# Zero products ahead of the first image, and one step of the last half image moved from VectorE to Pool

## The chip, the cores and the metric

The kernel is one program on one core of a Trainium2 chip. The metric is the time of one execution on the device in microseconds (us); the median of several executions is compared. The names of the engines are those of the profile: PE (TensorE matmul) with PEld (its weight loads), DVE (VectorE), ACT (ScalarE), POOL (GpSimd) and SP (SyncE, which here only issues DMAs).

## The reference, cut to what matters

Four layers follow one another on x of shape (8, 512, 32, 32), in float32. The first layer's f and g products and its batch normalization over all eight images are the start of the program; the fourth layer is its end.

```python
# layer 0: the parts that the start of the kernel computes
f_x = relu(batchnorm(conv1x1(x, Wf, bf), gamma_f, beta_f)).reshape(b, MID, hw)   # MID = 64
g_x = relu(batchnorm(conv1x1(x, Wg, bg), gamma_g, beta_g)).reshape(b, MID, hw)
h_x = conv1x1(x, Wh, bh).reshape(b, MID, hw)
z = einsum('bcn,bcm->bnm', f_x, g_x)
attn = z / svd(z)[:, 0]
x = conv1x1(einsum('bnm,bcm->bcn', attn, h_x), Wv, bv) + x
# layer 1: group norm, attention over 1024 positions with 512 channels, projection, + x
# layer 2: attention over 1024 positions with 128 channels, projection, batchnorm, + x
# layer 3
a = sign(x + rsign_bias)
y = einsum('bchw,oc->bohw', a, sign(W) * mean(abs(W), axis=1))
s = batchnorm(y) + x
t = s - pr_shift
out = where(t > 0, t, pr_slope * t) + pr_bias
```

## The kernel before

An image is held as a tile `xt` of 128 partitions by 4 channel chunks by 1024 positions, 2 MB. Two such tiles exist (pool `x`, two buffers), so the load of the third image waits until PE is done with the first.

**The start.** f's and g's weights (`fg`, four DMAs of 64 KB) are issued on ACT's queue, the first image on SP's queue (`load_x(0, True)`, line 141: its first chunk in two halves of 256 KB, three chunks of 512 KB), then h's weights on ACT's queue (line 156). `ident` and other constants follow: Pool makes `ident`, DVE derives masks from it (lines 178 to 195), and ACT's queue loads a table `ct` of small vectors (line 201), from which DVE computes scales (lines 243 to 248 and 1309 to 1326).

In the loop over the eight images (line 1370) PE multiplies the f, g and h weights, 64 columns each, with the image: `products(i, cc)` (line 1382) takes weight set i and channel chunk cc, and puts the two halves of the positions side by side on the partitions of one PSUM bank. For the first image the chunks come outermost, and each chunk is used for f and g as it lands; h follows. Every such product of the code stands as two passes in the trace. The results go to SBUF by ACT (f, line 1401, and h, line 1410) and DVE (g, line 1404). PSUM has two wide tiles and four banks here (`psum_pools(early, 2, 4)`); `bank()` hands the four out in turn.

Within this loop a scheduler orders each engine's instructions by readiness in its own model of time, starting from the order of the text; `tc.keep_in_program_order(ins)` pins an instruction behind the one that precedes it in the text on the same engine. On PE the stretch after the loop is ordered by hand (`manual_schedule`).

**The middle.** Each image then passes layers 1 to 3 in `fast`; the last image has a path of its own at the end.

**The tail.** `leave` computes layer 3, for halves h = 0 and h = 1 of the positions. ACT takes the signs of the half's four chunks (line 720), PE multiplies them with the weights' signs (line 732). For the last image `signs` holds the unpacked signs; then each j in 0, 1 gives two pieces of 128 channels by 512 positions, `y1` (channels oc = j) and `y2` (oc = j + 2). DVE forms y = product x scale + x (line 753). From there two forms exist:

- for h = 0, and for j = 0 of h = 1: DVE takes `up` = max(y, nc3) x ps3 (line 759), ACT overwrites y with slope x y + bias (line 762), Pool adds the two (line 769), SP sends y out (line 770). ACT's overwriting waits until line 759 has read y.
- for j = 1 of h = 1: ACT takes a Relu into `up` (line 775) and the scaled y (line 776), DVE joins them (line 783), SP sends them out (line 787); the last piece goes in two halves.

Of the kernel before, what the change touches and what calls it, by code (L numbers as in the profile page):

```python
# [8 lines left out]
F32 = mybir.dt.float32  # L9
# [7 lines left out]
P = 128  # L17
# [70 lines left out]
def kernel(  # L88
# [17 lines left out]
    nc = tc.nc  # L106
    mm = nc.tensor.matmul
# [17 lines left out]
    def bank():  # L125
        return psum["bank"].tile([P, HF], F32, tag="bank", name="bank")
# [9 lines left out]
    def load_x(b, split=False):  # L136
        t = xpool.tile([P, CC, N], F32, tag="x", name="xt")
        src = x[b].rearrange("(cc p) n -> p cc n", p=P)
        for cc in range(CC):
            for ns in [half(h) for h in range(NH)] if split and not cc else [slice(0, N)]:  # L140
                nc.sync.dma_start(out=t[:, cc, ns], in_=src[:, cc, ns])
        return t

    def half(i):
        return bass.ts(i, HF)

    def side(i):

        return slice(i * MID, (i + 1) * MID)
# [4 lines left out]
    def load_w(name, src, shape, pool=wpool, eng=nc.sync, tag=None):  # L154
        t = pool.tile(shape, F32, tag=tag or name, name=name)
        eng.dma_start(out=t, in_=src)
        sbw[name] = t
        return t
# [4 lines left out]
    a1 = early.enter_context(tc.tile_pool(name="a1", bufs=1))  # L163
    fg = sbw["fg"] = a1.tile([P, CC, P], F32, tag="fg", name="fg")
    for cc in range(CC):
        nc.scalar.dma_start(out=fg[:, cc, :], in_=w_fg[:, cc, :])
    first = load_x(0, True)
    load_w("h", w_h, [P, CC, MID], a1, nc.scalar)


# [64 lines left out]
    def col(name, i):  # L235
        return ct[:, COL[name] + i : COL[name] + i + 1]
# [476 lines left out]
    def leave(env, xt, dst, halves=range(NH), signs=None, stop=False):  # L713


        small = env["small"]
        for h in halves:
            sg = env["e"].tile([P, CC, HF], F16, tag="e", name="sg")
            for cc in range(CC):
                nc.scalar.activation(  # L720
                    sg[:, cc, :], xt[:, cc, half(h)], AF.Sign, bias=rb3[:, cc : cc + 1]
                )
            if stop:
                yield
            for j in range(CC // 2):
                both = env["e"].tile([P, 2, HF], F32, tag="e", name="both")
                y1, y2 = both[:, 0, :], both[:, 1, :]

                def product(lt):
                    ps = bank()  # L730
                    for cc in range(CC):
                        mm(  # L732
                            out=ps,
                            lhsT=lt[:, cc, bass.ts(j, P)],
                            rhs=sg[:, cc, :],
                            start=cc == 0,
                            stop=cc == CC - 1,
                        )
                    return ps

                if signs is None:
                    ps = product(sw3)
                    nc.scalar.activation(y2, ps, AF.Identity, bias=round3, scale=1.0 / PACK)
                    nc.vector.tensor_scalar(y2, y2, ROUND, None, ALU.subtract)
                    nc.vector.scalar_tensor_tensor(y1, y2, -PACK, ps, ALU.mult, ALU.add)
                    sums = y1, y2
                else:
                    sums = [product(signs[0])]
                    yield
                    sums.append(product(signs[1]))  # L750

                for y, ps, oc in ((y1, sums[0], j), (y2, sums[1], j + 2)):
                    nc.vector.scalar_tensor_tensor(
                        y, ps, sa3[:, oc : oc + 1], xt[:, oc, half(h)], ALU.mult, ALU.add
                    )
                    up = small.tile([P, HF], F32, tag="half_a", name="up3")
                    if signs is not None and (h == 0 or j == 0):

                        nc.vector.tensor_scalar(
                            up, y, nc3[:, oc : oc + 1], ps3[:, oc : oc + 1], ALU.max, ALU.mult  # L760
                        )
                        nc.scalar.activation(
                            y,
                            y,
                            AF.Identity,
                            bias=qb3[:, oc : oc + 1],
                            scale=col("L3_conv_pr_slope", oc),
                        )
                        nc.gpsimd.tensor_tensor(y, y, up, ALU.add)
                        nc.sync.dma_start(out=dst[:, oc, half(h)], in_=y)  # L770
                        continue
                    final = signs is not None and y is y2
                    for q in (slice(0, HF // 2), slice(HF // 2, HF)) if final else [slice(0, HF)]:
                        yq, uq = y[:, q], up[:, q]
                        nc.scalar.activation(uq, yq, AF.Relu, bias=cb3[:, oc : oc + 1])
                        nc.scalar.activation(
                            yq,
                            yq,
                            AF.Identity,
                            bias=pb3[:, oc : oc + 1],  # L780
                            scale=col("L3_conv_pr_slope", oc),
                        )
                        nc.vector.scalar_tensor_tensor(
                            yq, uq, ps3[:, oc : oc + 1], yq, ALU.mult, ALU.add
                        )
                        to = slice(h * HF + q.start, h * HF + q.stop)
                        nc.sync.dma_start(out=dst[:, oc, to], in_=yq)
                yield
# [551 lines left out]
    def load_blocks(name, src, parts):  # L1340

        if name not in sbw:
            sbw[name] = a1.tile([P, 4, GROUPS, QUAD], F32, tag=name, name="blocks_" + name)
        t = sbw[name]
        of = src.rearrange("(r a) c o -> r a c o", a=QUAD)
        for q in range(4):
            for r in parts:
                nc.sync.dma_start(
                    out=t[bass.ts(q, QUAD), r].rearrange("a (c m) b -> a c (m b)", c=CC),
                    in_=of[r][:, :, bass.ts(q, P)],  # L1350
                )
# [18 lines left out]
    for b in range(B):  # L1370
        xt = load_x(b) if b else first
        for name, src, pool in later.get(b, ()):
            load_w(name, src, shapes.get(name, [P, CC, C]), pool)
        if b in (2, 3, 4, 5):
            load_blocks(*((("q", w_q), ("k", w_k))[b // 2 - 1]), ((0, 1), (2, 3))[b % 2])
        if b >= B - 2:
            resident[b] = xt
        banks = [bank() for _ in w0[: 3 if b < B - 2 else 2]]

        def products(i, cc):  # L1380
            for h in range(NH):
                mm(  # L1382
                    out=banks[i][side(h), :],
                    lhsT=w0[i][:, cc, :],
                    rhs=xt[:, cc, half(h)],
                    start=cc == 0,
                    stop=cc == CC - 1,
                )

        if b == 0:  # L1390
            for cc in range(CC):
                for i in range(2):
                    products(i, cc)
        for i in range(3):
            if i == 2 and b >= B - 2:
                continue
            if b or i == 2:
                for cc in range(CC):
                    products(i, cc)
            if i == 0:  # L1400
                nc.scalar.copy(fs[b], banks[i])
                nc.vector.bn_stats(st[:, 0, b, :], fs[b])
            elif i == 1:
                nc.vector.tensor_copy(gs[b], banks[i])
                nc.vector.bn_stats(st[:, 1, b, :], gs[b])
                if last is not None:
                    turn(last[0], last[1], ht_pair[last[0] // 2], 0)
        if b < B - 2:
            hraw = a2.tile([P, HF], F32, tag="hraw", name="hraw")
            nc.scalar.activation(hraw, banks[2], AF.Identity, bias=bhc)  # L1410
            last = b, hraw
        else:
            last = None
        if b == 3:
            total3 = sign_weights()
        if b == 5:
            scale_signs(total3)
        if b > 5:
            natural(*((("q", "w3"), ("k", "q"))[b - 6]))
# [165 lines left out]
    with tc.manual_schedule(engines={mybir.EngineType.PE}):  # L1585
# [7 lines left out]
        ps = bank()  # L1593
# [6 lines left out]
        ps = bank()  # L1600
# [233 lines left out]
```

## Time and profile before

| what | us |
|---|---|
| four runs | 1872.57 to 1873.49, median 1873.09 |
| the profiled execution | 1873.44 |
| its span, first to last instruction | 1871.7 |
| PE busy | 1851.9 |
| DVE busy | 1121.6 |
| ACT busy | 542.0 |
| POOL busy | 121.9 |
| first product of the first image (line 1382) | starts at 4.53 |
| end of the last line 783 | 1867.1 |

How to read it: the page gives the busy time of every engine as a share of the span, and the chain of work that ended last, followed back from the last instruction: 96% of that chain is PE. The view in order of time lists instructions with start and length in us, merged where like ones follow one another, and in brackets the engine's idle time before them with what ended it; "issue" there is idle time that no wait in the profile explains. The same chain of waits can be had as a list in order of time. A windows view adds up each engine's busy time and the bytes moved in chosen stretches.

### The profile page before, as it was taken

Reading aid. Unit: us, or ns where it says so; the run is one execution under the profiler, and the core shown is the slowest. Engines: PE = TensorE matmul, PEld = TensorE weight load, DVE = VectorE, ACT = ScalarE, POOL = GpSimd, SP = SyncE. Lnnn points to the kernel's source line nnn. Section 1 sums busy time; section 2 is a strip of 40 time slices with the busy share of each in tenths; the row PEclk is TensorE's granted clock in tenths of the full one; section 3 lists DMA queues with packets and bytes.
Section 4 is the critical chain, followed back from the end, with each engine's and each line's share of the span. In section 5 each row is a group of like instructions: output and inputs, shape, how many; then the busy total and the mean of one; then the engine's idle time right before and its main releaser. Section 6 shows DMA issues by size and latency. Waiting matters only on the chain.

```text
span 1871.7 us, 16535 instructions
## 1 busy us (share of the span) xinstructions
PE 1851.9 (99%) x6196; PEld 947.9 (51%) x6196; DVE 1121.6 (60%) x2083; ACT 542.0 (29%) x882; POOL 121.9 (7%) x109
## 2 busy tenths in 40 slices
PE   9999999999999999999999999999999999999997
PEld 3365464544645465544645455544645464544653
DVE  3356677567754667567754776357643666355447
ACT  2042221244213521244202521244203521244114
POOL 1000001000010001100020001100010001000011
PEclk9999999999999999999999999999999999999999
DMA  8620000002000200002000200001000200000001
GB/s 276 206 87 7 1 18 1 1 34 73 12 1 12 90 17 1 0 35 73 12 1 12 90 18 0 1 34 68 12 0 12 90 12 0 1 34 23 12 0 47
DMA packets 32738, 66.52 MB, mean 36 GB/s; under 512 B 4944, under 2 KB 12300, under 8 KB 32524
## 3 DMA queue, kind: packets, MB, share of 16 engines
q1 hardware_dynamic: 31724, 64.96, 10.2%
q8 instruction: 51, 0.84, 0.2%
q10 hardware_dynamic: 864, 0.43, 0.1%
q14 instruction: 35, 0.29, 0.1%
q0 software_dynamic: 64, 0.00, 0.0%
HBM read 46.44 MB, written 18.94 MB: 35 GB/s over the span
## 4 chain that ended last, share of the span: by engine, by line
PE 96%; DVE 2%; ACT 1%; issue 0%; DMA 0%; POOL 0%; ACTq 0%; DVEq 0%
PE bank L413 46%; PE bank L591 21%; PE bank L993 6%; PE bank L840 6%; PE bank L1382 4%; PE bank L692 3%; PE bank L709 3%; PE bank L732 1%; PE bank L437 1%; PE wide L1428 1%; PE bank L1061 1%; PE bank L1486 1%; PE quad L1274 0%; PE bank L863 0%; DVE st L449 0%; DVE xt L446 0%
## 5 line engine op out<-in xcount | busy, mean ns | idle before, releaser
L591 PE MATMUL bank<-e,vt 128*128 128x512 f32 x768 | 336.2, 594 | 0.0
L591 PEld LDWEIGHTS bank<-e,vt 128*128 128x128 f32 x768 | 144.3, 190 | 172.3 <-issue 167.9
L413 PE MATMUL bank<-ut,h 128*128 128x512 f32 x384 | 178.9, 597 | 0.0
L413 PEld LDWEIGHTS bank<-ut,h 128*128 128x128 f32 x384 | 71.2, 190 | 94.7 <-issue 93.0
L413 PE MATMUL bank<-us,hs 128*128 128x512 f32 x256 | 115.6, 593 | 0.0
L840 PE MATMUL bank<-tpg 128*128 128x512 f32 x256 | 115.4, 595 | 0.0
L993 PE MATMUL bank<-e,tpg 128*128 128x512 f32 x256 | 114.7, 595 | 0.0
L364 DVE TENSOR_TENSOR e<-bank,e 128x512 f32<-128x512 f32 x96 | 66.2, 689 | 60.8 <-PE bank L413 45.1
L847 ACT ACTIVATE e<-bank 128x512 f32<-128x512 f32 x128 | 76.3, 597 | 67.0 <-PE bank L840 66.9
L358 ACT COPY e<-bank 128x512 f32<-128x512 f32 x96 | 56.1, 585 | 118.9 <-PE bank L413 118.5
L413 PE MATMUL bank<-wo,h 128*128 128x256 f32 x384 | 89.9, 384 | 0.0
L413 PE MATMUL bank<-h,wu 128*128 128x512 f32 x192 | 89.0, 594 | 0.8 <-DVE h L488 0.8
L244 POOL TENSOR_TENSOR r_r<-r_v,minus_half 128x4 f32<-128x4 f32 (+1 forms) x11 | 10.9, 989 | 1042.7 <-DVE r_v L243 1037.4
L993 PEld LDWEIGHTS bank<-e,tpg 128*128 128x128 f32 x256 | 48.1, 190 | 60.4 <-issue 60.0
L413 PEld LDWEIGHTS bank<-wo,h 128*128 128x128 f32 x384 | 71.4, 190 | 12.6 <-issue 3.8
L413 PEld LDWEIGHTS bank<-us,hs 128*128 128x128 f32 x256 | 48.4, 190 | 57.5 <-issue 54.5
L852 DVE TENSOR_TENSOR esum<-esum,e 128x1024 f32<-128x1024 f32 x48 | 58.8, 1225 | 30.1 <-ACT e L847 29.9
L840 PEld LDWEIGHTS bank<-tpg 128*128 128x128 f32 x256 | 47.6, 190 | 55.0 <-issue 52.4
L720 ACT ACTIVATE sg<-xt,rb 128x512 f16<-128x512 f32 x64 | 44.2, 716 | 107.4 <-DVE xt L711 104.5
L364 DVE TENSOR_TENSOR vt<-bank,vt 128x512 f32<-128x512 f32 x48 | 33.2, 692 | 66.4 <-PE bank L413 65.6
L358 ACT COPY vt<-bank 128x512 f32<-128x512 f32 x64 | 37.4, 584 | 121.3 <-PE bank L413 121.2
L358 ACT COPY ut<-bank 128x512 f32<-128x512 f32 x48 | 28.1, 586 | 127.9 <-PE bank L413 127.9
(361 smaller groups left out, 2916.8 us busy)
## 6 DMA issues: line engine op xcount, KB each, us to landing
xt<-in_x SPq DMA_DIRECT2D x55, 512.0 KB
out<-both SPq DMA_DIRECT2D x63, 256.0 KB
rfull<-r_dram SPq DMA_DIRECT2D x15, 512.0 KB
f_dram<-f SPq DMA_DIRECT2D x8, 256.0 KB
fb<-f_dram SPq DMA_DIRECT2D x8, 256.0 KB
w<-in_w SPq DMA_DIRECT2D x1, 1024.0 KB
blocks_q<-in_w_q SPq DMA_DIRECT2D x16, 64.0 KB
blocks_k<-in_w_k SPq DMA_DIRECT2D x16, 64.0 KB
```

Source lines behind the costliest of these rows:

```text
L358: nc.scalar.copy(dst, ps)
L364: nc.vector.tensor_tensor(dst, ps, u, ALU.add)
L413: mm(out=ps[:, q * w : (q + 1) * w], lhsT=lt(ka, kb, q, k), rhs=rhs(ka, kb, q, k), start=first and q == 0 and k == 0, stop=last and k == 1 ...
L591: mm(out=ps, lhsT=a[:, t, bass.ts(r_, P)], rhs=e[t], start=first and t == 0, stop=last and t == NTH - 1, skip_group_check=True,)
L692: mm(out=ps[:, i, :], lhsT=xt[:, cc, bass.ts(4 * h + i, P)], rhs=sbw["tpg"][:, cc, 2 * P : 3 * P], start=cc == 0, stop=cc == CC - 1,)
L709: mm(out=ps, lhsT=sbw["z"][:, bass.ts(oc, P)], rhs=att, start=True, stop=True)
L720: nc.scalar.activation(sg[:, cc, :], xt[:, cc, half(h)], AF.Sign, bias=rb3[:, cc : cc + 1])
L840: mm(out=ps, lhsT=pt[:, 0, bass.ts(t, P)], rhs=tt[:, 0, half(h)], start=True, stop=True,)
L847: nc.scalar.activation(e[:, half(h)], ps, AF.Exp, scale=float(P) ** -0.5)
L852: nc.vector.tensor_tensor(esum, esum, e, ALU.add)
L993: mm(out=banks[h], lhsT=gt[:, t, :], rhs=es[t][:, half(h)], start=t == 0, stop=t == NT - 1,)
L1382: mm(out=banks[i][side(h), :], lhsT=w0[i][:, cc, :], rhs=xt[:, cc, half(h)], start=cc == 0, stop=cc == CC - 1,)
```

## The change

Three edits.

- After the first image's load has been issued, a tile `still` of 128x128 is set to zero on DVE, a PSUM bank is taken, and PE multiplies `still` with itself fifteen times into it. Nothing reads the bank. The tile takes 512 bytes of each partition.
- In the tail the max-and-multiply of line 759 goes to Pool where h = 1, that is for the two pieces of j = 0 of the last image's second half; for h = 0 it stays on DVE.
- The first product of the first image (f, chunk 0, first half) is pinned behind PE's preceding instruction in the text, which is the last of the fifteen.

```diff
     first = load_x(0, True)
+    still = a1.tile([P, P], F32, tag="still", name="still")
+    nc.vector.memset(still, 0.0)
+    ps = bank()
+    for _ in range(15):
+        nc.tensor.matmul(out=ps[:, 0:P], lhsT=still, rhs=still, start=True, stop=True)
     load_w("h", w_h, [P, CC, MID], a1, nc.scalar)
...
                     if signs is not None and (h == 0 or j == 0):
 
-                        nc.vector.tensor_scalar(
+                        eng = nc.gpsimd if h else nc.vector
+                        eng.tensor_scalar(
                             up, y, nc3[:, oc : oc + 1], ps3[:, oc : oc + 1], ALU.max, ALU.mult
                         )
...
             for h in range(NH):
-                mm(
+                one = mm(
                     out=banks[i][side(h), :],
                     lhsT=w0[i][:, cc, :],
                     rhs=xt[:, cc, half(h)],
                     start=cc == 0,
                     stop=cc == CC - 1,
                 )
+                if b + i + cc + h == 0:
+                    tc.keep_in_program_order(one)
```

## The prediction

> **What bounds the kernel now.** I read the page first, then the order of time at both ends, then the chain of waits of the last 30 us. The page says that one engine sets the time almost everywhere:
>
> ```profile
> span 1871.7 us, 16535 instructions
> PE 1851.9 (99%) x6196; PEld 947.9 (51%) x6196; DVE 1121.6 (60%) x2083; ACT 542.0 (29%) x882; POOL 121.9 (7%) x109
> ```
>
> PE is busy in 99% of the span, so only work ahead of its first product, PE's own pace, and the stretch behind its last product can move the end. The change touches just these. The start, in the order of time (start, length, engine, line, operation, count, idle before):
>
> ```profile
> 4.53 10.31 PE L1382 MATMUL bank<-xt,fg 128*64 128x512 f32 x32 [4.53 <-DMA fg<-in_w_fg]
> 5.21 0.46 PEld L1382 LDWEIGHTS bank<-xt,fg 128*64 128x64 f32 x3 [0.39 <-DMA xt<-in_x]
> 8.68 0.41 PEld L1382 LDWEIGHTS bank<-xt,fg 128*64 128x64 f32 x2 [0.44 <-issue]
> 9.53 0.41 PEld L1382 LDWEIGHTS bank<-xt,fg 128*64 128x64 f32 x2 [0.44 <-issue]
> 10.38 0.24 PEld L1382 LDWEIGHTS bank<-xt,fg 128*64 128x64 f32 x2 [0.44 <-issue]
> 10.82 0.23 PEld L1382 LDWEIGHTS bank<-xt,fg 128*64 128x64 f32 x2 [0.20 <-issue]
> 8.99 0.24 DVE L243 TENSOR_SCALAR r_v<-ct 128x4 f32<-128x4 f32 x2 [8.99 <-DMA ct<-in_cols]
> 14.34 1.02 PE L1382 MATMUL bank<-xt,h 128*64 128x512 f32 x3
> ```
>
> Two weight loads, so two passes of a product, start every 0.85 us until 10.38 us and every 0.43 us from there: PE runs at half pace for 5.85 us after its first product (4.53 us). The granted clock is no help here, since the windows view gives 1.00 from the start; the spacing is the witness. Later images take 10.45 us for 48 passes in the chain of waits, 0.2177 us each. The 32 passes for the first f and g would take 32 x 0.2177 = 6.97 us at that pace; they take 14.34 - 4.53 = 9.81. So 2.84 us is all that a full clock at 4.53 us could save. DVE does nothing until 8.99 us.
>
> The end, as the chain of waits of the last stretch has it (start, length, what):
>
> ```profile
> 1858.68 0.55 DVE up L759
> 1859.28 0.67 DVE both L753
> 1860.04 0.55 DVE up L759
> 1860.59 0.72 DVE both L753 x2
> 1861.31 0.52 issue
> 1861.83 1.40 DVE up L759
> 1863.23 0.67 DVE both L753
> 1863.98 0.80 ACT both L776
> 1864.78 0.80 ACT up L775 x2
> 1865.58 0.50 ACT both L776
> 1866.60 0.48 DVE both L783
> ```
>
> PE's last product ends near 1861.7 us; from there DVE, then ACT, set the end at 1867.08, and 4.6 us of output transfer and closing follow. The reader should see the last L759: DVE sits for 0.52 us and then takes 1.40 us for what is 0.55 elsewhere, beside Pool's additions:
>
> ```profile
> 1860.15 2.79 POOL L769 TENSOR_TENSOR both<-both,up 128x512 f32<-128x512 f32 x2 [2.75 <-ACT both L762]
> ```
>
> **The head.** Added: one DVE memset of 128x128, fifteen products of 128 columns, a pin that keeps the first real product behind them, and one of four PSUM banks, free again long before the ring comes back to it (cost nothing; without that cover the second image's first product would wait). The memset goes onto the idle DVE. Engines begin at 0.74 us (first DMA issues); nearest rows for the memset are 0.22 us (Pool's memset of gm, 128x128) and 0.22 (DVE L182, 128x128). With a handover of 0.04 (the chain's "issue" steps are 0.02 to 0.07) PE starts its zeros at s = 1.0 us.
>
> What do fifteen cost? The nearest row of that shape, all at full pace:
>
> ```profile
> 1810.78 7.31 PE L692 MATMUL bank<-tpg,xt 128*128 128x128 f32 x64
> 1810.78 7.11 PEld L692 LDWEIGHTS bank<-tpg,xt 128*128 128x128 f32 x63 [0.24 <-issue]
> ```
>
> This is 32 products in the code and 64 passes in the trace, 7.11 / 63 = 0.113 us a pass. So fifteen products are 30 passes: 3.39 us at full pace. At the half pace (0.85 / 0.43 = 1.98) a pass is 0.223, and all thirty 6.70 us. That exceeds the 3.53 us between 1.0 and 4.53. If the pace again doubles 5.85 us after PE's first work, at 6.85 us, then 5.85 / 0.223 = 26.2 passes are through; the other 3.8 take 0.43, and the real products start at 7.28 instead of 4.53. They then run at full pace: 7.28 + 6.97 = 14.25 against 14.34. The head gains 0.1 us: what the clock gives back is spent on passing the zeros. The answer hardly depends on the wait, because both sums move by half of it. With a wait of 3.4 us in both kernels, for example, they give 13.04 against 11.50 + 1.70 = 13.20.
>
> Only unequal waits part them. Bounds: full pace from the first zero, so that they end at 1.0 + 3.39 = 4.39, ahead of the data: minus 2.84. Zeros that don't raise the pace at all: 1.0 + 6.70 = 7.70, then the same slow start as now, 9.81 more: 17.51, plus 3.17. I take minus 0.1, by the L692 row, whose shape is the same. The four times before spread over 0.92 us (1872.57 to 1873.49), which such unequal waits would explain.
>
> The Trainium skill, "TensorE: Matmul & The Clock Gate", Part 1, says that the array starts at half clock and is released after one full busy window of about 3.4 us, and that the windows run free of the kernel. The measured 5.85 us fits between one window and two. By that rule the wait is 3.4 to 6.8 us, drawn afresh in each run, and the head differs by minus 1.3 to plus 0.4 us against the profiled execution; the mean is about the same as above. The rule speaks against fifteen: the budget is one of time, and half-pace zeros overrun it.
>
> Cover for the data: the four pieces of x, with f's and g's weights, are 2.4 MB; the windows view adds up to 2.3 MB moved by 9.0 us and 2.6 by 10.0, while the last piece is needed at 7.28 + 3 x 1.74 = 12.5 us. In the early case it is needed at 9.75, so a stall there stays under 0.3 us. The loads of the third image are issued when PE frees the buffer (18.31 us now), so they move with PE, not against it.
>
> **The tail.** Of the last image's second half, the two j = 0 pieces move L759 from DVE to Pool: DVE loses 0.55 and 0.52 + 1.40 us, and Pool gains two operations. Pool has no such row. Below: its memset, 0.22 us for 128 columns, 0.5 for 512 if 0.1 of it is fixed (0.10 for one column). Above: the 1.26 us of its two-input addition L769, or 1.84 where that meets DVE (L630). I take 0.92, by the one-input affine select: 0.1 + 4 x (0.305 - 0.1).
>
> Placed by readiness: DVE does the first y to 1859.95, the second to 1860.7, and with no L759 between, the j = 1 pieces' L753 end at 1861.5 and 1862.4 (PE delivers at 1860.8 and 1861.7), 1.5 us earlier than 1863.90. Pool: first L759 1860.03 to 1860.95; the addition of the first half's last piece, ready at 1860.1 and now queued behind it, to 1862.2; second L759 to 1863.2; two additions to 1864.5 and 1865.8 (now 1865.4). New waits stand on ACT: L762 overwrites what L759 reads, so it now waits for Pool, to 1860.95 and 1863.2, and behind it on ACT wait L775 and L776 of the j = 1 pieces. If ACT holds today's order, its second L762 ends at 1864.0, the four remaining steps need 2.5 us, and the last L783 ends near 1867.0: nothing gained. If L776 goes ahead of that L762, 0.6 is gained. SP's output issues of the second piece come 0.4 us later; the last transfer still sets the end. I take minus 0.2. Bounds: minus 1.2 (Pool at 0.5: ACT held once, to 1860.55, then its own 4.8 us of work and a last L783 of 0.5, to 1865.9) and plus 1.8 (Pool at 1.84 with today's ACT order: second L759 to 1865.0, L762 to 1865.8, then 2.5 us and L783).
>
> The Trainium skill, "SBUF — State Buffer", Who interferes with whom, says that Pool and DVE share a port pair as an exclusive lock, also where DVE reads two SBUF inputs. The 1.40 us row agrees, and so does L783 at 1.16 beside L769 against its usual 0.75. By this rule the move cures L759 but may hold the final L783 behind Pool's later additions, up to 0.7 us worse than my sum.
>
> **Sum.** -0.1 - 0.2 = -0.3 us. The profiled execution took 1873.44 (span 1871.7 and 1.7 around it), which is 0.35 above the median of 1873.09; against it the sum gives 1873.1, against the median 1872.8. About 0.2% (3.75 us) is what counts as told apart here, so my forecast is no change.
>
> **Rivals.** Early clock: the zeros run near 0.113 us a pass or the release comes within a microsecond, and the head keeps its 2.84. With the tail between minus 0.2 and minus 1.2 that is 1869.0 to 1870.1. For it: the real products double their pace, so something releases it. Against: nothing in the trace runs at full pace in PE's first 5.85 us.
>
> Late zeros (the slower side): DVE's queue today opens with L243, which waits for a DMA until 8.99 us. If the memset stands behind it, PE is pinned to zeros that can't start before 9.3: at a 5.85 us wait they end at 15.6, products at 22.55, plus 8.2 us: 1881. It decides as soon as the memset isn't first; past a start of 5 us it would cost over 0.2%. Against: it needs no input, while L243 does.
>
> Slow Pool: L759 on Pool over 1.84 us; each extra microsecond costs two. At 3 us the tail loses about 4: 1877. Against: every one-input row on Pool is cheap.
>
> Zeros without effect: the pace isn't raised by them; plus 3.2, so 1876.0. Against: the weight loads and passes are the same instructions.
>
> **Chances.** No change as summed 0.66; early clock 0.14, a little over half of it beyond 0.2%; late zeros 0.09; slow Pool 0.07, half beyond; zeros without effect 0.04, about half beyond. So faster 0.08, slower 0.09 + 0.035 + 0.025 = 0.15, within 0.77. The time is the likeliest case's, 1872.8. The range takes the head's and the tail's bounds most of the way, 1870.0 to 1876.0; outside it are late zeros, part of slow Pool and part of early clock.
>
> **What would show it.** Head: PE's first pass near 1.0 us; passes of zeros 0.22 apart, then 0.11; the first L1382 product near 7.3 and the first h product near 14.2. A first product at 4.5 proves early clock; a first pass after 9 us, late zeros; half pace after the zeros, zeros without effect. Tail: L759 on Pool at 0.9 us, the j = 1 pieces' L753 done by 1862.4, ACT waiting for Pool ahead of L762, and the last L783 0 to 0.6 us earlier counted from PE's last product. I am wrong if either end moves by over 3 us.

## The result, and the profile after

The change is slower: the ratio to the kernel before is 1.0015, 95% interval 1.0011 to 1.002. The median is 1875.59 us (37 runs, 1874.67 to 1876.54) against 1872.74 (57 runs, 1871.71 to 1873.82), so 2.85 us more. The time lies in the forecast's range, but the forecast, no change with a small gain, is wrong. The profiled execution took 1875.22 us, its span is 1873.4.

In the changed kernel line 759 of before is 765, 753 is 758, 762 is 768, 769 is 775, 775 and 776 are 781 and 782, 783 is 789, 770 and 787 are 776 and 793, and 1382 is 1388. The page:

```profile
span 1873.4 us, 16591 instructions
PE 1854.2 (99%) x6226; PEld 947.7 (51%) x6226; DVE 1120.0 (60%) x2082; ACT 542.0 (29%) x882; POOL 125.4 (7%) x111
```

PE has 30 more passes and Pool 3.5 us more work. The start, in the order of time:

```profile
0.82 0.17 DVE L169 MEMSET still<- 128x128 f32 x1 [0.82 <-PEq L1832]
1.04 5.53 PE L172 MATMUL bank<-still 128*128 128x128 f32 x30 [1.04 <-DVE still L169]
6.50 7.09 PE L1388 MATMUL bank<-xt,fg 128*64 128x512 f32 x32
13.42 3.60 PE L1388 MATMUL bank<-xt,h 128*64 128x512 f32 x16
```

The zeros begin at 1.04 us and hold the first real product until 6.50 (before: 4.53). From there PE runs at full pace without a break, and h begins at 13.42 instead of 14.34. So the head gained 0.9 us in this execution. PE's last product ended 1.1 us earlier than before, at 1860.6 (1861.7). All the loss lies behind it. The chain of waits there (start, length, what):

```profile
1858.14 0.67 DVE both L758
1859.00 0.71 POOL up L765
1861.06 1.26 POOL both L775
1862.32 2.06 POOL up L765
1864.41 0.02 ACT both L768
1865.13 0.54 ACT up L781
1865.74 0.49 ACT up L781
1866.24 1.20 ACT both L782 x2
1867.43 0.41 ACT up L781
1867.87 0.61 ACT both L782
1868.50 0.48 DVE both L789
...
```

Where the chain before ran over DVE, it now runs over Pool and then over ACT. The two engines in the order of time, Pool first:

```profile
1859.00 2.09 POOL L765 TENSOR_SCALAR up<-both,nc,ps 128x512 f32<-128x512 f32 x1 [2.75 <-DVE both L758]
1861.06 1.26 POOL L775 TENSOR_TENSOR both<-both,up 128x512 f32<-128x512 f32 x1
1862.31 2.07 POOL L765 TENSOR_SCALAR up<-both,nc,ps 128x512 f32<-128x512 f32 x1
...
1861.12 0.81 ACT L768 ACTIVATE both<-both,qb,ct 128x512 f32<-128x512 f32 x1 [2.18 <-POOL up L765]
1864.41 0.81 ACT L768 ACTIVATE both<-both,qb,ct 128x512 f32<-128x512 f32 x1 [2.48 <-POOL up L765]
```

A max-and-multiply takes 2.08 us on Pool where DVE took 0.55 to 1.40. ACT waits for both (the brackets: 2.18 and 2.48 us), and all of its six steps for the j = 1 pieces stand behind the second wait, though DVE's last y was ready by 1861.4. DVE's last step ends 8.40 us after PE's last product; before it was 5.35.

### The profile page after: what moved, and what is told of

Its sections match the earlier page's. It is cut to its first block, busy times and chain, and to the rows that moved or that the text cites. A ratio compares the mean times of both kernels' runs of the same rounds, so it can differ in the third digit from the quotient of the medians.

```text
span 1873.4 us, 16591 instructions
## 1 busy us (share of the span) xinstructions
PE 1854.2 (99%) x6226; PEld 947.7 (51%) x6226; DVE 1120.0 (60%) x2082; ACT 542.0 (29%) x882; POOL 125.4 (7%) x111
## 4 chain that ended last, share of the span: by engine, by line
PE 96%; DVE 2%; ACT 1%; issue 0%; POOL 0%; ACTq 0%; DVEq 0%; POOLq 0%
PE bank L418 46%; PE bank L596 21%; PE bank L999 6%; PE bank L846 6%; PE bank L1388 4%; PE bank L697 3%; PE bank L714 3%; PE bank L737 1%; PE bank L442 1%; PE wide L1436 1%; PE bank L1067 1%; PE bank L1494 1%; PE quad L1280 0%; PE bank L869 0%; DVE st L454 0%; DVE xt L451 0%
```

## The experiments

Each run was timed against the kernel before on the same chip. A single run's ratio has an interval of about 0.09% to either side, 1.7 us, so smaller differences rest on the traces. "Tail" below is the stretch from PE's last product to the end of the span, worked out from each trace: 9.94 us before, 12.85 after. Traces of runs that share a tail agree within 0.2 us, but for one pair that differs by 0.6 (named below).

**The two halves alone.**

```diff
# zeros only: the head of the change, tail as before
+    for _ in range(15):
+        nc.tensor.matmul(out=ps[:, 0:P], lhsT=still, rhs=still, start=True, stop=True)
# Pool only: the tail of the change, head as before
+                        eng = nc.gpsimd if h else nc.vector
+                        eng.tensor_scalar(
```

> The change's head alone: fifteen products of zeros and the pin, tail as before. Theory A (the loss is in the tail): the zeros cost what the clock gives back, so the time is 0.1 to 0.6 us below before, and the first h product starts within 1.3 us of 14.3 us. Rival B (the zeros hold the real products back for more than they save): 1 to 3 us above before, and most of the change's 2.85 us is here.

> The change's tail alone: the two max-and-multiply steps on Pool, no zeros. Theory A: all of the loss and a little more, 3.0 us above before; on Pool each of the two takes 2.08 us, ACT waits over 2 us for each, and the last L783 ends 3.0 us later counted from PE's last product. Rival B: under 1.5 us above before.

Zeros only: 1872.56 against 1873.05, minus 0.49 (ratio 0.9997, 0.9988 to 1.0006). Its sign can't be told from these times, but a loss of more than 1.1 us lies outside the interval: rival B falls but for its lowest edge. In the trace h starts at 12.94, 1.4 us sooner than before. Pool only: 1876.01, plus 2.96 (1.0015, 1.0006 to 1.0024), with a tail of 13.03 us and DVE's last step 3.0 us later behind PE's last product, as theory A has it. The two add up to plus 2.47; the change measured plus 2.85. The loss is the tail's.

**How many zeros.**

```diff
-    for _ in range(15):
+    for _ in range(8):       # in the other run: range(30)
```

> Eight products of zeros in place of fifteen, tail as before. Theory A (a product of zeros takes 0.427 us until the pace doubles): sixteen passes of 0.213 us from 1.04 us end at 4.45 us, just before the data of the first image, so they delay nothing and 3.5 us of the slow time are spent on zeros: 1.7 us below before and about 1.5 us below the run with fifteen. Rival C (the pace doubles a fixed time after the first real product, or only after more zeros than this): within 0.4 us of before.

> Thirty products of zeros in place of fifteen, tail as before: the suspected cost doubled. Theory A (zeros past the data's arrival stand on PE's path at their full-pace price): 30 passes more by 0.112 us, 3.3 us above the run with fifteen, 2.8 us above before. Rival C (they fill time that PE would spend slow or waiting for data): within 0.7 us of the run with fifteen.

Thirty: 1875.96 against 1872.87, plus 3.09, and 3.6 above fifteen (each against its own before). Doubling the zeros brought about the price that theory A names, 3.3 us; C falls. PE's rows of that run:

```profile
1.06 9.78 PE L172 MATMUL bank<-still 128*128 128x128 f32 x60 [1.06 <-DVE still L169]
10.77 7.09 PE L1387 MATMUL bank<-xt,fg 128*64 128x512 f32 x32
```

The data of the first product were there long before 10.77 (before, it started at 4.53); the real products simply stand behind the zeros.

Eight: 1872.05 against 1873.05, minus 1.0, where A expected 1.7 and C at most 0.4 either way; these times can't part them. The real products take over at 4.77 (A: 4.45, ahead of the data at 4.53), and h starts at 12.83, 1.51 us sooner than before, not 2.84. The rows of the weight loads (PEld) show what A left out:

```profile
5.68 0.52 PEld L1387 LDWEIGHTS bank<-xt,fg 128*64 128x64 f32 x2 [0.33 <-issue]
6.37 0.28 PEld L1387 LDWEIGHTS bank<-xt,fg 128*64 128x64 f32 x2 [0.16 <-issue]
...
9.35 0.20 PEld L1387 LDWEIGHTS bank<-xt,fg 128*64 128x64 f32 x4 [0.98 <-DMA xt<-in_x]
...
11.02 0.24 PEld L1387 LDWEIGHTS bank<-xt,fg 128*64 128x64 f32 x4 [0.62 <-DMA xt<-in_x]
```

First the pace: eight zeros ended before it doubled, so the first four real passes, 4.77 to 6.37, took 1.59 us instead of 0.86. Then the data. The brackets are idle time of the weight loads and not of PE: of the 1.6 us, PE's products lost only 0.41, at 9.35, and nothing at the second wait. But the image's last piece was there only at 11.02, and its eight passes take 1.72 us at full pace. So h could not have started before 12.74, however early the pace had doubled: of the 2.84 us that a full pace would have saved, the data's arrival leaves at most 1.6 in this execution. In the later run with eight zeros and two buffers PE itself waited for that piece, until 11.25:

```profile
11.25 1.94 PE L1393 MATMUL bank<-xt,fg 128*64 128x512 f32 x8 [0.40 <-DMA xt<-in_x]
```

**Freeing ACT.** ACT gets a buffer for the scaled y, so that it needn't wait for Pool's reading; then the j = 1 pieces get one for the Relu.

```diff
# ACT's own buffer
+                        ys = small.tile([P, HF], F32, tag="half_b", name="ys") if h else y
                         nc.scalar.activation(
-                            y,
+                            ys,
                             y,
...
-                        nc.gpsimd.tensor_tensor(y, y, up, ALU.add)
+                        nc.gpsimd.tensor_tensor(y, ys, up, ALU.add)
# two buffers: as well
+                    if signs is not None and h and j:
+                        if y is y1:
+                            ups = small.tile([P, 2, HF], F32, tag="esum", name="ups", bufs=1)
+                        up = ups[:, 0 if y is y1 else 1, :]
```

> The change's tail, but ACT writes the scaled y of these two pieces to a buffer of its own, so it no longer waits for Pool to have read y; no zeros. Theory A (the loss is Pool's 2 x 2.08 us and, on top, ACT's steps for the j = 1 pieces queued behind that wait): the last L783 ends earlier than before's, Pool's last addition sets the end, 3 x 1.26 + 2 x 2.08 us after the first y, and the time is 0.5 to 1.4 us above before. Rival D (ACT's order has no part in it, Pool's length and the port alone cost it): 3 us above before, as with the shared buffer.

> As the run with Pool and ACT's own buffer, but the two j = 1 pieces of the last half also take the Relu into a buffer of their own instead of the ring of three that Pool's additions release. Theory A2 (ACT was tied to Pool twice, by the overwritten y and by the ring of three): ACT no longer waits for Pool at all, its last step ends before Pool's, Pool's five operations one behind the other set the end, and the time is 1.0 to 1.8 us above before, at least 1 us below the run with the one buffer. Rival D (Pool's length and the port alone): still 2.6 to 3.0 us above before.

The first gave 1875.87 against 1873.05, plus 2.82 (1.0015, 1.0006 to 1.0024): a miss. The wait removed was replaced by another, as ACT's rows of that run show; the Relu (L777) takes a buffer from a ring of three that Pool's additions release:

```profile
1860.24 1.66 ACT L764 ACTIVATE ys<-both,qb,ct 128x512 f32<-128x512 f32 x2
1863.70 0.72 ACT L777 ACTIVATE up<-both,cb 128x512 f32<-128x512 f32 x1 [1.79 <-POOL both L771]
...
1867.20 0.91 ACT L777 ACTIVATE up<-both,cb 128x256 f32<-128x256 f32 x2 [1.94 <-POOL both L771]
```

The second gave 1875.74 against 1873.07, plus 2.67 (1.0015, 1.0006 to 1.0024): a miss again in the time. ACT no longer waits for Pool and DVE is done at 1864.32, 1.5 us sooner behind PE's last product than before. The rows of that run, SP's last, say why this bought nothing:

```profile
1863.35 0.97 DVE L790 SCALAR_TENSOR_TENSOR both<-ups,ps,both 128x256 f32<-128x256 f32 x2 [0.54 <-ACT both L783]
...
1864.73 2.48 POOL L776 TENSOR_TENSOR both<-ys,up 128x512 f32<-128x512 f32 x2
...
1867.66 1.71 SPq L794 DMA_DIRECT2D out<-both  x3
```

The three finished outputs (L794) are issued from 1867.66, 3.3 us after the last of them was computed: they stand in SP's queue behind the output that waits for Pool's last addition.

**SP's order.** The two outputs that wait for Pool are issued last.

```diff
-                        nc.sync.dma_start(out=dst[:, oc, half(h)], in_=y)
+                        if h:
+                            sent.append((oc, y))
...
+                if j:
+                    for oc, y in sent:
+                        one = nc.sync.dma_start(out=dst[:, oc, half(h)], in_=y)
+                        tc.keep_in_program_order(one)
```

> As the run with Pool and two buffers, but SP issues the two outputs that wait for Pool behind the three of the j = 1 pieces instead of ahead of them; no zeros. Theory A3 (after ACT's two ties the third is SP's queue: three finished outputs stood behind the ones that wait for Pool): those three leave from 1863 on, only the two 256 KB outputs come after Pool's end, and the time falls by 0.7 to 1.6 us against that run, to 1.2 to 2.1 us above before: what is left is Pool's own length. Rival D: unchanged, 2.6 to 3.0 us above before.

1874.99 against 1872.87, plus 2.12 (1.0011, 1.0002 to 1.002), at the upper edge of theory A3. The tail fell from 12.77 to 11.79 us, by the expected size; the times fell by 0.55, less than the 0.7 expected, and can't show so small a step. With all three ties cut, Pool's five operations in a row remain. Its last row:

```profile
1865.86 2.47 POOL L777 TENSOR_TENSOR both<-ys,up 128x512 f32<-128x512 f32 x2
```

The last addition ends 6.70 us after PE's last product (1861.64), where before everything was computed at 5.35.

**The same buffers with the work on DVE.** The control of the runs above; in a further run DVE's second max-and-multiply is pinned behind the last L753.

```diff
# late max: the second j = 0 piece, held until the j = 1 pieces are scaled
+                        if late3:
+                            tc.keep_in_program_order(top)
```

> The same two buffers, but with the max-and-multiply on DVE as before; no zeros. Theory A2 (ACT's steps of the j = 1 pieces stood behind waits for L759): ACT is free from 1861.3 on, only the last y at 1863.9 holds it, and the time is 0.5 to 1.0 us below before. Rival E (DVE's chain to the last y, with the L759 of 1.40 us in it, sets the end anyway): within 0.3 us of before.

> As the run just before, and DVE's second L759 of the last half is pinned behind the last L753, so that the step that Pool's addition holds back no longer stands ahead of the last y. Theory A2: the last y is there at 1862.4 instead of 1863.9 (frame of before), ACT works without a gap, and the time is 1.2 to 1.8 us below before. Rival E': the second piece, now later, ends last by way of Pool's addition: within 0.5 us of before.

Two buffers: 1872.48, minus 0.59 (0.9989 to 1.0007), with DVE's last step 0.76 us nearer to PE's last product, as theory A2 has it; the times can't part A2 from rival E. The traced tail is 9.13 us, but 9.71 in the run with eight zeros below, which shares this tail and has DVE's last step just as early: the final outputs can take most of that gain back. Against the same buffers with the work on Pool (plus 2.67) the move costs 3.3 us.

Late max: 1872.81, minus 0.26, tail 9.98. The time is the one that rival E' gives, but not quite by its reason, since Pool's last addition was done at 1864.14 and DVE ended last:

```profile
1862.87 1.27 POOL L791 TENSOR_TENSOR both<-ys,up 128x512 f32<-128x512 f32 x1 [0.48 <-DVE up L778]
1863.26 2.27 DVE L805 SCALAR_TENSOR_TENSOR both<-ups,ps,both 128x512 f32<-128x512 f32 x3 [0.53 <-ACT both L798]
```

The three joins (L783 before, L805 here) took 2.27 us together, the first of them beside Pool's addition, and SP's three last issues followed one another.

**Pool's price.**

```diff
+            nc.gpsimd.tensor_tensor(pb, pa, pa, ALU.add)
+            nc.gpsimd.tensor_scalar(pb, pa, one, two, ALU.max, ALU.mult)
+            nc.gpsimd.tensor_scalar(pb, pa, one, None, ALU.max)
+            nc.gpsimd.tensor_scalar(pb, pa, two, None, ALU.mult)
+            nc.gpsimd.tensor_scalar(pb, pa, 0.5, 2.0, ALU.max, ALU.mult)
+            nc.gpsimd.tensor_scalar(pb, pa, one, two, ALU.add, ALU.mult)
+            nc.gpsimd.tensor_scalar(pb[:, 0:256], pa[:, 0:256], one, two, ALU.max, ALU.mult)
```

> Before, with seven forms on Pool, three times each, on a tile of its own at a time when Pool has nothing else: an addition of two tiles, max-and-multiply with per-partition scalars (the change's form), max alone, multiply alone, max-and-multiply with constants, add-and-multiply with per-partition scalars, and the change's form on 256 columns. Theory A: the change's form takes 2.08 us without anything beside it, so the price is the form's own; two steps cost more than one, and 256 columns take a little over half. Rival F (the 2.08 us came from DVE on the shared port): near 1 us here.

The groups by shape on Pool, lines 1660 to 1666 in the order of the diff, here by cost (count, total and mean ns):

```profile
L1661 POOL TENSOR_SCALAR pb<-pa,nc,ps 128x512 f32<-128x512 f32 x3 | 6.2, 2077 | 0.3
L1664 POOL TENSOR_SCALAR pb<-pa 128x512 f32<-128x512 f32 x3 | 5.8, 1929 | 0.3
L1663 POOL TENSOR_SCALAR pb<-pa,ps 128x512 f32<-128x512 f32 x3 | 4.7, 1564 | 0.3
L1662 POOL TENSOR_SCALAR pb<-pa,nc 128x512 f32<-128x512 f32 x3 | 4.7, 1560 | 0.3
L1666 POOL TENSOR_SCALAR pb<-pa,nc,ps 128x256 f32<-128x256 f32 x3 | 3.6, 1212 | 0.3
L1660 POOL TENSOR_TENSOR pb<-pa 128x512 f32<-128x512 f32 x3 | 3.1, 1039 | 0.2
L1665 POOL TENSOR_SCALAR pb<-pa,nc,ps 128x512 f32<-128x512 f32 x3 | 2.3, 764 | 0.3
```

The change's form takes 2.077 us here as in the tail: the price is the form's, rival F falls. (The time of this run, 1889.35 us once, holds the added work and is not compared.) The operation pair decides: add-and-multiply with the same operands takes 0.764.

**Towards a better kernel.** Eight zeros with the two buffers on DVE; then eight zeros with the cheap form on Pool and ACT doing the Relu, so that DVE has no part of either.

```diff
# cheap form, for h = 1
+                            nc.scalar.activation(
+                                up, y, AF.Relu, bias=pc3[:, oc : oc + 1], scale=ps3[:, oc : oc + 1]
+                            )
+                            nc.gpsimd.tensor_scalar(
+                                ys, y, dv3[:, oc : oc + 1], slope, ALU.add, ALU.mult
+                            )
# pc3 = ps3 x cb3; dv3 = pb3 / slope
```

> Eight zeros and the tail with the two buffers and max-and-multiply on DVE: the two edits that came out below before, together. If they add: 1.0 + 0.6 = 1.6 us below before, 4.4 us below the change. If the head's gain is eaten later: 0.6 below before.

> Eight zeros, the two buffers, and another split of the two j = 0 pieces of the last half: ACT takes the Relu of the scaled y, Pool the add-and-multiply that takes 0.76 us there instead of the max-and-multiply of 2.08, then the addition; DVE has neither. If the form's price is what made the move dear: DVE's last y is there at 1862.4 (frame of before), Pool's last addition ends near 1865.4 as before, and the time is 1.0 to 1.4 us below before in the tail, 1.8 to 2.4 with the eight zeros. If any work on Pool costs there: no better than eight zeros alone, 1.0 below before.

Eight zeros with two buffers: 1871.65 against 1872.87, minus 1.22 (0.9985 to 1.0003), between the two outcomes that were expected, 1.6 and 0.6, and not to be told from either. The cheap form: 1872.38, minus 0.49, a miss by over a microsecond; it is no better than eight zeros alone. DVE had its last y early as expected, but look at the two ends of that run, DVE first and then SP:

```profile
1861.34 3.21 DVE L806 SCALAR_TENSOR_TENSOR both<-ups,ps,both 128x512 f32<-128x512 f32 x3 [0.77 <-ACT both L799]
...
1860.94 2.93 POOL L792 TENSOR_TENSOR both<-ys,up 128x512 f32<-128x512 f32 x2
...
1864.32 1.98 SPq L810 DMA_DIRECT2D out<-both  x3
```

Three joins that take 0.75 and twice 0.48 alone took 3.21 us beside Pool's additions, and SP issued the last three outputs from 1864.32 on, behind Pool's. Whether the issues or the transfers set that end was tried with ACT as the issuer of the last three outputs, there and as a control on the run with eight zeros and two buffers:

```diff
+                for oc, to, yq in sent:
+                    one = nc.scalar.dma_start(out=dst[:, oc, to], in_=yq)
+                    tc.keep_in_program_order(one)
```

> As the run with the cheap form on Pool and eight zeros, but the three outputs of the j = 1 pieces are issued by ACT, which has nothing left to do, instead of by SP behind the outputs that wait for Pool. In that run DVE's last step ended 0.6 us sooner after PE's last product than in before, yet the end came 0.9 us later, with SP's last issues 0.6 us apart. Theory S (SP's queue of issues sets the end once the computing is out of the way): the last issue comes within 0.9 us of DVE's last step and the time falls by 0.8 to 1.6 us. Rival T (the transfers themselves, bunched at the end, set it): within 0.4 us of that run.

> The same move of the three outputs to ACT's queue, on the run with eight zeros and max-and-multiply on DVE. Theory S: there SP's last issues followed DVE's last step within 0.4 us, so little is to be had, 0 to 0.5 us below that run. Rival T: no change.

The first: 1871.81 against 1872.94, minus 1.13; against before it is 0.64 better than from SP, and the tail fell from 10.82 to 10.09 us. Its rows, DVE first and then ACT:

```profile
1861.51 3.21 DVE L807 SCALAR_TENSOR_TENSOR both<-ups,ps,both 128x512 f32<-128x512 f32 x3 [0.78 <-ACT both L800]
...
1862.95 2.27 ACTq L816 DMA_DIRECT2D out<-both  x3
```

The last issue ends 0.5 us behind DVE's last step, as theory S has it, and 1.25 us sooner behind PE's last product than from SP, but the end came only 0.73 us sooner. The time's 0.64 lies between S's 0.8 and T's 0.4 and is not clear of noise, so how the end divides between the issues and the transfers stays open. The control: 1871.38 against 1872.94, minus 1.56 (0.9992, 0.9983 to 1.0001), 0.3 better than from SP against before, with a traced tail of 9.42 against 9.71: within what S allows, and no test against T. This is the lowest median of all runs, 4.2 us under the change; against before, its interval still just reaches no difference.

## Why the prediction was wrong

**The step that failed** is the price of line 759 on Pool: "I take 0.92, by the one-input affine select", with 1.84 as the upper end. It is 2.08, above the upper end. The neighbours were chosen by the number of inputs, and the cost goes by the pair of operations: add-and-multiply would have cost 0.76.

**ACT's order.** The sum took a middle between "ACT holds today's order" and the better one, minus 0.2. The order on the chip was worse than either: all steps of the j = 1 pieces stood behind the second wait, six in the trace, where the sum had four remaining (the trace of before has five behind its second L762). The rule that went with the slow case, two microseconds for each one on Pool, gives 1.8 + 2 x 0.24 = 2.3 us for 2.08; DVE's last step came 3.04 us later behind PE. The rival "slow Pool" is what happened. It had a chance of 0.07, because "every one-input row on Pool is cheap", and those rows were memsets and a select. That the time still lies in the range is luck: the tail alone went past its own bound of plus 1.8 (Pool only: plus 2.96), and the room for it came from the head's bound of plus 3.17.

**The head was right** in mechanism: the zeros gave back about what they cost, and the sum of minus 0.1 can't be told from the measured minus 0.49. The zeros started at 1.04 us (predicted 1.0), their passes were 0.213 us apart and then 0.112 (0.223 and 0.113), and full pace came during them. The wait for full pace was 4.0 us there against 5.85 before, and half of that difference is the 0.9 us by which this execution's head gained; the wait was 2.8 to 6.0 over all the profiled executions with zeros or without. Early clock, zeros without effect and late zeros are all excluded by the rows of the change. Thirty zeros confirmed the price.

**The early clock** was priced at 2.84 us with "a stall there stays under 0.3 us" for the data. The term went by the bytes moved, which had the last piece needed at 9.75 and there within 0.3 us of it. In the three runs with eight zeros whose weight loads waited for it, it came at 10.68 to 11.25, 0.9 to 1.5 us later than needed. With its eight passes of 1.72 us behind it, that leaves 1.4 to 1.9 of the 2.84 us.

**The cover of SP** was passed over: "SP's output issues of the second piece come 0.4 us later". They came 2.5 us later behind PE's last product, and whatever was done stood behind them in that queue. It was hidden by ACT's lateness in the change itself and became the bound once ACT was freed.

**The port** was weighed as up to 0.7 us at the last L783. In the change DVE's last steps ran free of it, since Pool was done before them. Joins that took longer beside Pool's additions are seen in the late-max and cheap-form runs instead; that the port is the reason was not tested on its own.

## What to carry to other kernels

An operation moved to another engine has to be priced by its exact pair of operations there, and measured where no such row exists. Before freeing one wait, list every tie between the slow step and the end: here the overwritten input, a ring of buffers that the slow engine releases, and the output queue, and cutting the first two alone gained nothing that could be measured. Warming work ahead of the data is free only until the data arrive; beyond that each piece costs at least its full-pace price, and the saving ends where the loads do. And an idle time of the weight loads is not one of PE: only the starts of the products tell what was lost.

## What the runs showed of the hardware

- On Pool, 128x512 in float32 takes 2.08 us as max-and-multiply, 1.56 as max or as multiply alone, and 0.76 as add-and-multiply: two operations can be cheaper than one.
- PE's full pace came 3.0 us after its first work in the run with zeros only and 6.0 us in the run with outputs last. The Trainium skill, "TensorE: Matmul & The Clock Gate", Part 1, asks for a full busy window of about 3.4 us and has the change around 4 us into sustained work, within 0.5 us to either side; the 2.99 us measured (full pace at 4.05, first zero at 1.06) is below that and the 6.0 us above, and where they differ the measurement decides.
- An output's issue on SP took 0.33 us in the change for those that stood alone; the last three of the cheap-form run, one behind another, took 0.38, 1.03 and 0.38.
